# Layernorm's 1/sd by three Newton steps on GpSimd in place of ScalarE's square root, with half of efficient attention's applies on ScalarE

## Chip, cores and metric

The kernel runs on one core of one Trainium2 chip. The metric is the device time of one execution in microseconds, as the median of three runs. A core has a matrix engine (TensorE, PE in the profile), a vector engine (VectorE, DVE), an engine for activation functions (ScalarE, ACT), a general engine (GpSimd, POOL) and a queue engine for transfers (SyncE, SP). Each engine works through its own queue of instructions in order, and waits on semaphores for the others.

## What is computed

The input x is 8 batches of 512 tokens with 128 features. Six residual blocks follow one another, each behind a layernorm without weights:

```python
def _layernorm(x, axis=-1, eps=1e-05):
    m = jnp.mean(x, axis=axis, keepdims=True)
    v = jnp.var(x, axis=axis, keepdims=True)
    return (x - m) / jnp.sqrt(v + eps)

x = x + 0.5 * _L0_ffn_ref(_layernorm(x), ...)   # feed-forward, blockwise 4-bit values
x = x + _L0_attn_ref(_layernorm(x), ...)        # softmax attention, 16 heads of 64
x = x + 0.5 * _L0_ffn_ref(_layernorm(x), ...)   # the same feed-forward again
x = x + 0.5 * _L1_ffn_ref(_layernorm(x), ...)   # mixture of 8 experts, top 2
x = x + _L1_attn_ref(_layernorm(x), ...)        # efficient attention, 6 layers
x = x + 0.5 * _L1_ffn_ref(_layernorm(x), ...)   # the mixture again
```

Efficient attention is the stage that matters most here. Each of its six layers begins with a layernorm that has weights gamma and beta:

```python
for l in range(depth):
    residual = x
    h = _layernorm(x, gamma[l], beta[l])      # (x - mu) * rsqrt(var + 1e-5) * gamma + beta
    q, k, v = jnp.split(h @ w_qkv[l], 3, axis=-1)
    q = jax.nn.softmax(q, axis=1)             # over the tokens
    k = jax.nn.softmax(k, axis=2)             # over the features
    context = jnp.einsum('bic,bjc->bij', k, v)
    out = jnp.einsum('bic,bij->bjc', q, context) @ w_out[l] + b_out[l]
    x = out + residual
```

## The kernel before

All of x stays on the chip. Batch b is a tile xs[b] of 128 partitions by 4 chunks (NC) of 128 features: a token to a partition, four tokens a partition. The batches go in groups of four (GT). The six stages are functions that run in the order of the reference: ffn4, attention, ffn4, moe, linear_attention (the efficient attention), moe. The times of the stages in the profile are about 0 to 184, 184 to 1230, 1230 to 1369, 1369 to 1665, 1665 to 1971 and 1971 to 2271 us.

A scheduler arranges the instructions of an engine from their dependences and a cost model, so their order can differ from the order in the source. Tiles come from pools of a few buffers each; a tile with the same tag waits until the oldest buffer is free.

*Layernorm.* `ln_stats` (L152) takes the tiles of a group, 16 chunks in all. For each chunk VectorE makes the partial statistics st (bn_stats, L159) and from them mean and variance mv (bn_aggr, L161). Then one ScalarE instruction makes sd, the root of the variance plus eps (L163), and one VectorE instruction its reciprocal rstd (L165), each on 128x16. It is called 24 times: twice in each stage outside efficient attention, twice at the entry of efficient attention, and for each of its six layers and two groups. `ln_apply` (L168) then makes one VectorE instruction a chunk, 128x128: (x - mean) * rstd (L172), with the mean and rstd of each partition as operands.

ScalarE's functions live in tables. An ACT_TABLE_LOAD stands ahead of an instruction whose function isn't in the loaded one: ahead of Sqrt, of Exp, of the sigmoid functions.

*ffn4.* `hidden(t)` applies layernorm, quantizes xh (`quantize`, a chain on VectorE whose last multiplication, L214, is GpSimd's: x_xq, h_xq or w_xq), transposes it and makes the hidden values h. `down(t, h)` quantizes those and multiplies back. hidden(t + 1) is written ahead of down(t).

*attention.* A planner writes the order of TensorE's work by hand; `prepare(b)` makes a batch's layernorm and its transpose (L181), and GpSimd adds the bias bo to x (L322).

*moe.* The layernorm output mxh goes to memory, is gathered by GpSimd's indirect transfers for each expert, and the results are combined on VectorE.

*linear_attention.* `layer(l, batches, ys)` (L786) does one layer for one group of four batches; the layers run one after the other, the two groups in turn, so a group's layer is free to overlap with the other group's. This makes twelve layer-groups, here called periods. In each, for the four batches:

- xh is the applied layernorm (L172), 4 x 4 chunks; TensorE transposes it into ph (L798), ScalarE writes lhT with gamma and beta (L800), and GpSimd adds the output bias to y in place (L806), which must wait until xh has been read from y.
- TensorE multiplies to lpq (L812) and lpk (L825); VectorE takes the maxima nmq (L814) and nmk (L829); ScalarE's exponentials make eq (L817, 128x512) and ek (L833, 128x128 each).
- TensorE transposes eq (pqt, L845), VectorE scales it (eqt, L847), TensorE multiplies with ek to pm (L855), and VectorE scales that to mT (L859).
- A first round with w_out (pm2, L863) and a second with w_v (pm3, L868); behind each ScalarE copies the result, lm, out of PSUM (L865, L870), four copies a round.
- TensorE multiplies lhT with the second lm to lpo (L874, 16 instructions of two parts), and VectorE adds it to y (L877). In the last layer GpSimd adds y to x (L879).

The statistics of a group's next layer can begin once its y is added; its xh, ph and lpq follow while the other group is in its later steps. In the profile the y adds and the next ph of the group that is up stand side by side.

## Time and profile before

| what | value |
|---|---|
| median of 3 runs | 2272.65 us (2271.04 to 2274.14) |
| the profiled execution | 2272.8 us, its span 2271.1 us |
| instructions | 31365 |
| efficient attention, 1665 to 1971: PE, DVE, ACT, POOL busy | 268.9, 284.8, 194.3, 69.2 us of 306 |
| attention, 184 to 1230: PE, DVE, ACT, POOL busy | 1020.1, 675.3, 542.9, 46.7 us of 1046 |
| GpSimd's add of 128x512 (L806), 48 times | 1.286 us on average |
| GpSimd's scaling of x_xq 128x512 and h_xq 128x1408 (L214) | 1.341 and 2.684 us on average |
| VectorE's apply of 128x128 in efficient attention (L172), 192 times | median 0.338 us, up to 1.320 |

The span is the time from the first to the last instruction in the profile, and the execution's own time is 1.7 us more. In lines of the profile, "DVE L172 TENSOR_SCALAR xh<-y,mv,rstd 128x128 f32<-128x128 f32 x11" is eleven instructions of line 172 on VectorE that write xh from y, mv and rstd. In a timeline the first two numbers are the start and the busy time of a row in microseconds, and what stands in brackets at the end is how long the engine was idle before it and which instruction released it. In the view of one source line, the first row of each form has the shortest, median and longest duration in nanoseconds, with first and last start in microseconds. In the row of 40 slices each digit is the busy share in tenths; a slice is 56.8 us.

### The profile page before, as it was taken

Reading aid. Unit: us, or ns where it says so; the run is one execution under the profiler, and the core shown is the slowest. Engines: PE = TensorE matmul, PEld = TensorE weight load, DVE = VectorE, ACT = ScalarE, POOL = GpSimd, SP = SyncE. Lnnn points to the kernel's source line nnn. Section 1 sums busy time; section 2 is a strip of 40 time slices with the busy share of each in tenths; the row PEclk is TensorE's granted clock in tenths of the full one; section 3 lists DMA queues with packets and bytes.
Section 4 is the critical chain, followed back from the end, with each engine's and each line's share of the span. In section 5 each row is a group of like instructions: output and inputs, shape, how many; then the busy total and the mean of one; then the engine's idle time right before and its main releaser. Section 6 shows DMA issues by size and latency. Waiting matters only on the chain.

```text
span 2271.1 us, 31365 instructions
## 1 busy us (share of the span) xinstructions
PE 1869.2 (82%) x11321; PEld 1283.6 (57%) x11321; DVE 1509.5 (66%) x3392; ACT 946.5 (42%) x2439; POOL 467.3 (21%) x458
## 2 busy tenths in 40 slices
PE   2767999999999999999996755887439999859781
PEld 1544666665666566665664545654327777646560
DVE  8986756666575656666567994444379999745342
ACT  1324545555455545545451321232226767413230
POOL 1221000000000000000000220773332122227615
PEclk9888999999999999999998875797769999858885
DMA  6000000000000000000000001241100000013312
GB/s 175 1 0 1 1 1 1 1 1 1 1 1 1 1 1 1 1 1 1 1 1 1 1 0 37 56 93 48 48 18 1 1 1 1 20 35 74 85 58 65
DMA packets 57032, 47.61 MB, mean 21 GB/s; under 512 B 6512, under 2 KB 51760, under 8 KB 56880
## 3 DMA queue, kind: packets, MB, share of 16 engines
q1 hardware_dynamic: 46720, 26.16, 4.0%
q0 software_dynamic: 9216, 18.89, 3.8%
q8 instruction: 93, 1.52, 0.3%
q10 hardware_dynamic: 944, 0.54, 0.1%
q14 instruction: 59, 0.48, 0.1%
HBM read 28.80 MB, written 16.78 MB: 20 GB/s over the span
## 4 chain that ended last, share of the span: by engine, by line
PE 72%; DVE 14%; DMA 5%; issue 3%; POOL 3%; ACT 2%; POOLq 0%; DVEq 0%; ACTq 0%
PE pS L360 11%; PE pT L387 11%; PE po L402 10%; PE ph L690 5%; DMA yk<-yg,rows 4%; PE pym L714 3%; PE pq L332 3%; PE py L430 3%; PE pv L346 3%; PE pk L338 2%; PE ptok L629 2%; PE pm L855 2%; PE lpq L812 2%; PE lpo L874 2%; PE py L286 2%
## 5 line engine op out<-in xcount | busy, mean ns | idle before, releaser
L372 ACT ACTIVATE pe<-pS,nmax 128x512 f32<-128x512 f32 x512 | 348.7, 692 | 289.9 <-DVE nmax L369 216.3
L369 DVE TENSOR_REDUCE nmax<-pS 128x2 f32<-128x1024 f32 x256 | 302.0, 1218 | 131.6 <-PE pS L360 131.6
L392 DVE COPY aT<-pT 128x512 f32<-128x512 f32 x448 | 290.4, 684 | 97.5 <-PE pT L387 97.4
L387 PEld LDWEIGHTS pT<-ident,pe 128*128 128x128 f32 x2048 | 227.3, 141 | 86.6 <-issue 68.7
L387 PE MATMUL pT<-ident,pe 128*128 128x128 f32 x2048 | 273.1, 276 | 2.1 <-DVE aT L392 2.1
L360 PE MATMUL pS<-kT,qT 64*128 64x512 f32 x1024 | 256.4, 619 | 0.8 <-ACT pe L372 0.8
L402 PE MATMUL po<-aT,v 128*64 128x256 f32 x2048 | 249.6, 386 | 0.0
L414 POOL COPY wide<-rsum 128x512 f32<-128x512 f32 x64 | 39.3, 613 | 962.7 <-PE pT L387 903.8
L690 PE MATMUL ph<-wall,xgT 128*128 x320 | 166.3, 645 | 29.2 <-DVE g L696 21.7
L660 POOL DMA_INDIRECT xgs<-xg,toks x160 | 157.0, 981 | 157.7 <-DVE toks L634 109.5
L402 PEld LDWEIGHTS po<-aT,v 128*64 128x64 f32 x2048 | 136.2, 137 | 76.6 <-issue 21.3
L360 PEld LDWEIGHTS pS<-kT,qT 64*128 64x128 f32 x1024 | 88.6, 187 | 117.8 <-issue 109.4
L748 POOL DMA_INDIRECT yk<-yg,rows x128 | 120.9, 944 | 156.3 <-DMA yg<-ygs 111.0
L696 DVE TENSOR_TENSOR g<-g,ph 128x256 f32<-128x256 f32 x160 | 66.6, 419 | 112.3 <-ACT g L695 109.3
L695 ACT ACTIVATE g<-ph 128x256 f32<-128x256 f32 x160 | 60.9, 383 | 172.9 <-PE ph L690 172.9
L752 DVE SCALAR_TENSOR_TENSOR x<-yk,m,x 128x128 f32<-128x128 f32 x128 | 44.7, 353 | 118.6 <-DMA yk<-yg,rows 118.4
L806 POOL TENSOR_TENSOR y<-y,bout_sb 128x512 f32<-128x512 f32 x48 | 61.7, 1286 | 220.2 <-DVE xh L172 220.2
L372 ACT ACTIVATION_READ_ACCUMULATOR pe<-pS,nmax 128x1 f32 x512 | 105.8, 207 | 0.0
L690 PEld LDWEIGHTS ph<-wall,xgT 128*128 128x128 f32 x320 | 59.0, 207 | 79.9 <-issue 37.0
L277 PE MATMUL hqT_ps<-ident,h_xq 128*128 128x128 f32 (+1 forms) x192 | 35.1, 350 | 80.3 <-POOL h_xq L214 80.3
L798 PE MATMUL ph<-ident,xh 128*128 128x128 f32 x192 | 31.9, 295 | 72.6 <-DVE xh L172 72.5
L714 PE MATMUL pym<-wall,gT 128*128 x640 | 87.8, 296 | 1.4 <-DVE gT L707 1.4
(193 smaller groups left out, 3354.6 us busy)
## 6 DMA issues: line engine op xcount, KB each, us to landing
yg<-ygs SPq DMA_DIRECT2D x40, 256.0 KB, 2.4
xg<-mxh SPq DMA_DIRECT2D x16, 256.0 KB, 2.3
xgs<-xg,toks POOLq DMA_INDIRECT x160, 2.6
x<-in_x SPq DMA_DIRECT2D x8, 256.0 KB, 4.5
yk<-yg,rows POOLq DMA_INDIRECT x128, 2.5
out<-x SPq DMA_DIRECT2D x8, 256.0 KB, 2.5
wall<-in_w1T SPq DMA_DIRECT2D x1, 1024.0 KB, 9.2
wall<-in_w2T SPq DMA_DIRECT2D x1, 1024.0 KB, 11.5
```

The source lines that it names most:

```text
L332: nc.tensor.matmul(ps, wq_sb[:, cols(g)], hTs[g // NPAIR], start=True, stop=True)
L346: nc.tensor.matmul(ps[:, c, :], hT[:, c * P : (c + 1) * P], wv_sb[:, cols(g)], start=True, stop=True,)
L360: nc.tensor.matmul(ps[:, j, :], qTs[g][rows, c * P : (c + 1) * P], kTs[g][rows, :], start=True, stop=True,)
L369: nc.vector.tensor_reduce(nmax, ps, AX.X, ALU.max, negate=True)
L372: nc.scalar.activation(pe[:, j, :], ps[:, j, :], AF.Exp, bias=nmax[:, j : j + 1], accum_out=sums[g][:, 2 * c + j : 2 * c + j + 1],)
L387: nc.tensor.transpose(ps[:, k, :], pe[:, j, k * P : (k + 1) * P], ident)
L392: nc.vector.tensor_copy(dst, ps)
L402: nc.tensor.matmul(pos[g][rows, half * 2 * P : (half + 1) * 2 * P], vs[g][:, k, rows], aT[:, j, k, :], start=(k == 0), stop=(k == NC - 1),)
L660: nc.gpsimd.indirect_dma_start(x[:, s, :], None, xg[:, :], bass.IndirectOffsetOnAxis(ap=toks[:, q * QS + s : q * QS + s + 1], axis=0),)
L690: nc.tensor.matmul(ph.rearrange("p a h -> p (a h)"), xTs[q][:, s, :], wall[:, bass.ds(at, 2 * HID)], start=True, stop=True,)
L714: nc.tensor.matmul(py[:, s, :], gs[q][:, s, k, :], wall[:, bass.ds(ats[q * QS + s] + (2 * HID + k * D), D)], start=(k == 0), stop=(k == NH ...
L748: nc.gpsimd.indirect_dma_start(yk, None, yg[:, :], bass.IndirectOffsetOnAxis(ap=rows[:, j, k : k + 1], axis=0),)
```

## The change

The standard deviation's root and reciprocal go. In their place VectorE adds eps to the variance (v), shifts its bits to the right and subtracts them from a constant, which gives a first guess of 1/sqrt(v) by the form of floating-point numbers. GpSimd then multiplies v by -0.5 and does three Newton steps, each of four instructions on 128x16 that depend on one another: rstd = rstd * (1.5 - 0.5 * v * rstd * rstd). This is in `ln_stats`, so for all 24 layernorms. The tile eps, which was the bias of the root, goes too.

In efficient attention, a new function `ln_shift` makes -mean * rstd (one VectorE instruction on 128x16), and `ln_apply` gives every second chunk, 8 of the 16 of a group, to ScalarE as Identity with rstd as scale and the shift as bias. The applies of other stages stay on VectorE.

```diff
+RSQRT_GUESS = 0x5F3759DF
...
-    eps = const.tile([P, 1], F32, name="eps")
-    nc.vector.memset(eps, EPS)
...
-        sd = stat.tile([P, n], F32, name="sd", tag="sd")
-        nc.scalar.activation(sd, mv[:, :, 1], AF.Sqrt, bias=eps)
+
+        v = stat.tile([P, n], F32, name="v", tag="v")
+        nc.vector.tensor_scalar(v, mv[:, :, 1], EPS, None, ALU.add)
         rstd = stat.tile([P, n], F32, name="rstd", tag="rstd", bufs=3)
-        nc.vector.reciprocal(rstd, sd)
+        bits = stat.tile([P, n], I32, name="bits", tag="bits")
+        nc.vector.tensor_scalar(bits, v.bitcast(I32), 1, None, ALU.logical_shift_right)
+        nc.vector.tensor_scalar(rstd.bitcast(I32), bits, -1, RSQRT_GUESS, ALU.mult, ALU.add)
+        nc.gpsimd.tensor_scalar(v, v, -0.5, None, ALU.mult)
+        sq = stat.tile([P, n], F32, name="vsq", tag="vsq")
+        for _ in range(3):
+            nc.gpsimd.tensor_tensor(sq, rstd, rstd, ALU.mult)
+            nc.gpsimd.tensor_tensor(sq, sq, v, ALU.mult)
+            nc.gpsimd.tensor_scalar(sq, sq, 1.5, None, ALU.add)
+            nc.gpsimd.tensor_tensor(rstd, sq, rstd, ALU.mult)
         return mv, rstd
 
-    def ln_apply(dst, xt, stats, i):
+    def ln_shift(stats):
+
+        mv, rstd = stats
+        shift = stat.tile(rstd.shape, F32, name="shift", tag="shift")
+        nc.vector.scalar_tensor_tensor(shift, mv[:, :, 0], -1.0, rstd, ALU.mult, ALU.mult)
+        return shift
+
+    def ln_apply(dst, xt, stats, i, shift=None):
+
         mv, rstd = stats
         for c in range(NC):
             k = i * NC + c
+            if shift is not None and c % 2:
+                nc.scalar.activation(
+                    dst[:, c, :], xt[:, c, :], AF.Identity,
+                    bias=shift[:, k : k + 1], scale=rstd[:, k : k + 1],
+                )
+                continue
             nc.vector.tensor_scalar(
...
                 stats = ln_stats([ys[b] for b in batches])
+                shift = ln_shift(stats)
...
-                    ln_apply(xh, y, stats, i)
+                    ln_apply(xh, y, stats, i, shift)
```

## The prediction

> **What bounds the kernel now.** I read four views in order: the busy shares and slices of the page; the row of the square root with those who waited for it; the engines' timelines through one period of efficient attention, where half of the layernorms lie; and the chain of waits at the other layernorms.

> ```profile
> PE 1869.2 (82%) x11321; PEld 1283.6 (57%) x11321; DVE 1509.5 (66%) x3392; ACT 946.5 (42%) x2439; POOL 467.3 (21%) x458
> DVE  8986756666575656666567994444379999745342
> ACT  1324545555455545545451321232226767413230
> ```

> The shares average over six stages with different limits. Slices 30 to 34 are efficient attention (1665 to 1971 us): VectorE at 9, ScalarE at 6 to 7. There the change can act most.

> ```profile
> L163 ACT ACTIVATE sd<-mv,eps x24: 299/308/311, 17.1 to 1991.1; 128x16 f32<-128x16 f32 x24
> L163 ACT ACT_TABLE_LOAD  x20: 1283/1283/1283, 5.3 to 1961.1; - x20
>   DVE mv L161: 102.0, 19
>   PEld ph L798: 61.9, 1
>   DVE rstd L165: 5.4, 6
> ```

> 24 square roots of 0.31 us, with 20 table loads of 1.283 us. The last two lines list who waited: it is short, so most of these loads are not what another engine visibly waits for.

> Efficient attention runs twelve layer-groups, spaced 23.43 us (lpq at 1735.65 and 1759.08). ScalarE, VectorE and TensorE across the seam between two of them:

> ```profile
> 1747.46 1.28 ACT L163 ACT_TABLE_LOAD   x1
> 1749.41 0.31 ACT L163 ACTIVATE sd<-mv,eps 128x16 f32<-128x16 f32 x1 [0.67 <-DVE mv L161]
> 1750.17 0.27 ACT L865 COPY lm<-pm 128x128 f32<-128x128 f32 x1 [0.45 <-PE pm L863]
> ```
> ```profile
> 1750.21 0.24 DVE L165 RECIPROCAL rstd<-sd 128x16 f32<-128x16 f32 x1
> 1750.49 4.81 DVE L172 TENSOR_SCALAR xh<-y,mv,rstd 128x128 f32<-128x128 f32 x11
> 1755.23 0.68 DVE L877 TENSOR_TENSOR y<-lpo,y 128x512 f32<-128x512 f32 x1
> ```
> ```profile
> 1753.21 3.51 PE L874 MATMUL lpo<-lm,lhT 128*128 128x128 f32 x30
> 1758.65 0.59 PE L798 MATMUL ph<-ident,xh 128*128 128x128 f32 x2 [0.62 <-DVE xh L172]
> 1759.08 1.02 PE L812 MATMUL lpq<-lhT,wqkv_sb 128*128 128x512 f32 x2
> ```

> The period is a loop over three engines, and I cut it at E, the end of the last exponential (1747.44); S, the start of the long row of lpo (1753.21); and L, the next lpq (1759.08). E to S is 5.77, S to L 5.87, L to the next E 11.79 (23.43 in all). In E to S, the table load for the root ends at 1748.74, 0.67 before the last mean and variance (mv) is there: this load is hidden. The other load, back to exp at L817 (1737.79 to 1739.08), stands between the fourth lhT and the first exponential, and from there ScalarE runs without a gap to E: this load is on the path. VectorE applies eleven xh before the first y is added.

> [...]the trace has the 1.283[...] (load 1737.79, exponential 1739.08). [...]the new applies need no load; the trace's lm copies (L865) follow a root without one. [...]the trace has 1.06 us for 512 elements (x_xq) and 2.09 for 1120 (w_xq), 1.7 ns an element and 0.19 us at zero[...]. [...]a waiting ScalarE apply holds up the copies behind it.

> **The change part by part.** The profiled execution took 2272.8 (span 2271.1 and 1.7 around it), the median is 2272.65; so differences carry over as they are.

> *The price of a Newton step.* Each of the 24 calls of ln_stats gets three small VectorE operations (v, bits, guess), v times -0.5 on GpSimd beside bits and guess, and then 12 dependent GpSimd operations on 128x16. No row shows such an operation. From the slope: 0.19 + 16 x 0.0017 = 0.21 us; a hand-over from VectorE to GpSimd took 0.07 (y of L877 ended 1943.51, GpSimd began 1943.58), and I take the same for GpSimd waiting on itself: 0.28. Below: 0.20, when the dependent instruction's start overlaps its forerunner's end; the row of 32 numbers (iota) took 0.147. Above: 0.38, by the 128-element affine_select row (0.28) and a hand-over of 0.10. With 0.28 the chain is 12 x 0.28 = 3.36 (2.4 to 4.6); it replaces a root of 0.31 and a reciprocal of 0.24.

> *E to S, by the order in which the changed kernel issues.* mv is there at E+1.93, v at 2.13, the guess at 2.72 (an mT of 0.35 lies between), the Newton end at 6.08, shift (0.22) at 6.30. On ScalarE the first xh stands after the four copies of the first pm round and ahead of the four copies of the second, which lpo needs. So lpo now waits for Newton: hand-over 0.07, one xh spaced 0.33, one copy 0.27, hand-over 0.07: S = E+7.04, against 5.77: +1.27. The copies' own cover would last until E+5.8; what remains beyond it is the cost.

> *S to L.* Of 16 applies of a group ScalarE takes 8, so VectorE does six and not eleven ahead of the y adds, and they are done before the last lpo (3.51 after S). Then: hand-over 0.10, last y 0.67, one xh 0.34, hand-over 0.07, ph to lpq 0.38 (0.43 for two ph before): L = S+5.07, against 5.87: -0.80. What is late next is lpo itself. GpSimd's adds of bout_sb (1.29, L806) wait for both engines' applies; only the y adds wait for them, and they come later in this order.

> *L to E.* The load of 1.283 goes. Before, the first exponential began at L+3.43. Now nmq, which VectorE ended at L+1.75, allows it at L+1.8, but the fourth lhT (spaced 0.70) has moved inside the row of exponentials: 2.5 in its place, -0.9. So 10.9.

> Sum: +1.27 - 0.80 - 0.9 = -0.43 a period. Ten seams have it all: -4.3. The first and last layer-groups, which lose loads but have no full seam, -2 by estimate. GpSimd's 0.01 us more in price is 0.12 a period.

> *Outside efficient attention* (estimates from the rows around each layernorm; ScalarE applies nothing there):
> - First ffn4, group 0: Newton queues behind w_xq on GpSimd (16.84 to 18.93), rstd at 22.4 and not 19.2, of which 1.4 covers idle time: +2.2. Group 1: two loads and a root on ScalarE (68.14 to 71) go, Newton waits for h_xq (63.1 to 66.1): -1.
> - Attention's first layernorm (load at 161.11, on the chain): Newton behind the last h_xq, +1. Its second, at 719.5: two loads of 1.28 and a root stand on the chain of waits; GpSimd was idle for long, and TensorE has other heads' work: -2.
> - Second ffn4, group 1: h_xq holds GpSimd to 1260.3 and rstd was due at 1259.6, now 1263.6; one load saved: +2.5.
> - Entry to efficient attention +1 (Newton is exposed, but only half of layer 0's applies are VectorE's; 16 took 7.05 us). Mixture of experts: hidden in the first; +1.5 in the second pass, where mxh waits for GpSimd ahead of other VectorE work.

> Sum: 2.2 - 1 + 1 - 2 + 2.5 + 1 + 1.5 = +5.2. All: -4.3 - 2 + 5.2 = -1.1, so 2272 (2271.6). The three VectorE operations more a layernorm, against one reciprocal less, some 0.4 us, are in the times of v and guess; the applies taken off VectorE exceed them.

> **The rivals.** About six of the other layernorms and ten seams have Newton's 12 operations on the path: 16 x 12 = 192 operations, so 0.01 us of price is 1.9 us in all.

> *Newton is dearer* (the slower side): one mechanism, the GpSimd chain between mv and the lm copies, at 0.36 an operation, gives 192 x 0.08 = +15.4, so 2287. It decides from 0.31 up (1.9 x 3 - 1.1 = +4.6). For it: [...]small instructions above 0.2 in the trace (affine_select), and that GpSimd's 1.06 for 512 alone becomes 1.34 on average beside VectorE's work. Against it: memsets of one element took 0.10 to 0.12.

> *The loads and the split pay in full*: at 0.20 an operation E to S is 6.08, each seam gives 1.4, and all the rest shrinks too: -192 x 0.08 - 1.1 = -16.5, so 2256. For it: iota at 0.147; against it, the hand-over of 0.07.

> *The loads were hidden anyway*: if the first exponential waits for nmq or for TensorE, L to E gains only 0.3: +6 over ten seams, 2278. The row of exponentials without a gap behind the load speaks against it. I count it within the first case's own range.

> **How the numbers follow.** Break-even (2265 to 2279, by prices from 0.25 to 0.32): 0.45, and the likeliest, 2272. Newton dearer: 0.32. Paid in full: 0.23. About 0.2% (4.5 us) is what a measurement of this kernel tells from no change. Of the first case 0.14 falls below it, 0.21 within, 0.10 above; so faster 0.37, same 0.21, slower 0.42. The range reaches to 2256 and to 2290, which leaves a tenth out on each side; the first case's own is 2265 to 2279.

> **What would show it.** Table loads: 47 to 12, none left at a layernorm. GpSimd's 128x16 rows spaced 0.28, 24 x 13 of them. In a period: S at E+7.0, L at S+5.1, the first exponential 2.5 after L, and 23.0 as the spacing of lpq. The lm copies of the second round wait behind an xh that waits for shift, and lpo's idle is put down to them. ScalarE's apply 0.45 us; VectorE's applies 288 in place of 384. I am wrong if the Newton rows are spaced under 0.24 or over 0.32, if ScalarE's queue doesn't hold lpo, or if another stage moves by more than 4 us.

## The result and the profile after

The changed kernel takes 2294.38 us (median of 4 runs, 2292.7 to 2295.42), the kernel before, measured beside it, 2271.85. The ratio is 1.0099, with a 95% interval of 1.0082 to 1.0117: about 22 us slower. A second measurement (after_again) gave 2294.23 and 1.0086 (1.0069 to 1.0103). In the profiled executions the spans are 2291.0 and 2271.1, a difference of 19.9, which is what the traces have to explain.

The changed kernel has 12 table loads (1.283 us each) in place of 47, as forecast, and none of them is at the new applies. Its page has the shares and slices. The line of the square root is gone, and two views of lines in its place show the last GpSimd instruction of a Newton step and the shift that waits for it:

```profile
PE 1869.5 (82%) x11321; PEld 1293.8 (56%) x11321; DVE 1477.6 (64%) x3355; ACT 931.1 (41%) x2476; POOL 539.9 (24%) x770
DVE  8996666566666666666667983544377778645342
ACT  1224545455454545455451221332046666403230
```
```profile
L174 POOL TENSOR_TENSOR rstd<-vsq,rstd x72: 220/222/223, 20.6 to 2012.5; 128x16 f32<-128x16 f32 x72
L181 DVE SCALAR_TENSOR_TENSOR shift<-mv,rstd x12: 174/175/176, 1682.2 to 1957.8; 128x16 f32<-128x16 f32 x12
  POOL rstd L174: 38.3, 12
```

VectorE does 32 us less and ScalarE 15 less. Still efficient attention's slices have VectorE at 7 to 8 where they had 9. One cause is that half of the applies there have left VectorE. The last line shows the other: twelve times, once a layer-group, VectorE stood still for 3.2 us on average until the Newton chain had ended.

By landmarks the 19.9 us lie as follows; a "row of exponentials" is that of one layer-group, twelve in each kernel.

| stretch of the profiled execution, us | before | after | difference |
|---|---|---|---|
| up to the first mixture (first mxh) | 1369.50 | 1369.28 | -0.2 |
| first mixture, to its last write of x | 296.02 | 292.84 | -3.2 |
| entry of efficient attention, to the end of the first row of exponentials | 33.47 | 40.57 | 7.1 |
| from there to the end of the twelfth row | 262.07 | 275.04 | 13.0 |
| behind it | 310.04 | 313.24 | 3.2 |

The prediction had 3.7 ahead of the layers, -6.3 in them (some of this at their edges) and 1.5 behind. So most of the error lies in the seams between the layer-groups, and about 6 us more at the entry. There nothing covers Newton, twice, ahead of TensorE's first product of the stage: once for the entry's second layernorm, and once for layer 0's.

```profile
1671.52 4.19 DVE L195 TENSOR_SCALAR y<-x,mv,rstd 128x128 f32<-128x128 f32 x16 [2.22 <-POOL rstd L174]
1682.15 0.17 DVE L181 SCALAR_TENSOR_TENSOR shift<-mv,rstd 128x16 f32<-128x16 f32 x1 [2.21 <-POOL rstd L174]
```

The shorter mixture isn't shown to be the change's: e8_behind_copies and e15_behind_held below, with the same code there, have 296.06 and 296.43.

One seam of the changed kernel, with E (the end of the last exponential) at 1751.95. First the timeline of GpSimd and VectorE (start, busy time, engine, line, operation; in brackets the idle time ahead and its releaser):

```profile
1754.71 0.22 POOL L171 TENSOR_TENSOR vsq<-rstd 128x16 f32<-128x16 f32 x1
1755.00 0.22 POOL L172 TENSOR_TENSOR vsq<-vsq,v 128x16 f32<-128x16 f32 x1
1755.31 0.26 POOL L173 TENSOR_SCALAR vsq<-vsq 128x16 f32<-128x16 f32 x1
1755.65 0.22 POOL L174 TENSOR_TENSOR rstd<-vsq,rstd 128x16 f32<-128x16 f32 x1
...
1758.13 0.22 POOL L174 TENSOR_TENSOR rstd<-vsq,rstd 128x16 f32<-128x16 f32 x1
```
```profile
1758.38 0.17 DVE L181 SCALAR_TENSOR_TENSOR shift<-mv,rstd 128x16 f32<-128x16 f32 x1 [3.33 <-POOL rstd L174]
1758.48 1.62 DVE L195 TENSOR_SCALAR xh<-y,mv,rstd 128x128 f32<-128x128 f32 x6
1762.32 0.69 DVE L901 TENSOR_TENSOR y<-lpo,y 128x512 f32<-128x512 f32 x1 [2.22 <-PE lpo L898]
```

The twelve instructions from 1754.71 to 1758.35 are spaced 0.31 on average. Then the timelines of ScalarE and TensorE in the same seam:

```profile
1756.48 0.27 ACT L889 COPY lm<-pm 128x128 f32<-128x128 f32 x1 [0.35 <-PE pm L887]
1758.65 0.49 ACT L190 ACTIVATE xh<-y,shift,rstd 128x128 f32<-128x128 f32 x1 [1.91 <-DVE shift L181]
1759.05 0.41 ACT L894 COPY lm<-pm 128x128 f32<-128x128 f32 x2
```
```profile
1756.28 1.01 PE L892 MATMUL pm<-lm,wvT_sb 128*128 128x128 f32 x4
1759.35 1.23 PE L892 MATMUL pm<-lm,wvT_sb 128*128 128x128 f32 x4 [2.07 <-ACT lm L894]
1760.37 4.65 PE L898 MATMUL lpo<-lm,lhT 128*128 128x128 f32 x32
1766.32 1.13 PE L836 MATMUL lpq<-lhT,wqkv_sb 128*128 128x512 f32 x2
```

ScalarE's first xh waits 1.91 us, two lm copies stand behind it, and TensorE is idle for 2.07. Behind the copies it has first to make two more products of the second round (pm3 has two buffers, so they could not go ahead of the copies), and only then lpo. And the 32 instructions of lpo take 4.65 us. The view of windows (start and end, length, busy time of TensorE, its weight loads, VectorE, ScalarE and GpSimd; behind them TensorE's granted clock, DMA share, GB/s) has the same stretch and another seam of the same kernel, and in its third line all eleven seams of the kernel before:

```profile
1760.37:1765.00 4.63, 4.63 (x35) 4.63 (x35) 2.65 (x7) 1.89 (x6) 3.36 (x3) 0.79 0.01 4
1836.33:1840.00 3.67, 3.67 (x35) 3.67 (x34) 2.74 (x7) 2.01 (x6) 3.64 (x3) 1.00 0.00 0
1692.00:1960.00 268.00, 248.71 (x1717) 202.39 (x1717) 254.52 (x867) 183.03 (x634) 61.55 (x48) 1.00 0.00 1
```

35 matmuls take 4.63 us at a clock of 0.79 and 3.67 at 1.00. The clock is 0.50 for 3.4 us (6.8 in the first case) behind the wait in seven of the eleven seams (1732, 1760, 1787, 1811, 1886, 1910, 1961), and 1.00 in the other four, of which three have the same wait (the first seam has none). The kernel before has no seam with a lower clock. The distances between the ends of the exponentials follow this: 23.96 to 23.98 in three of the nine inner seams, 25.35 to 25.60 in five with the fall, 26.62 in one where it lasted longest; before, 23.42 to 23.56 in all nine.

| pieces of a seam, us | before | forecast | after, clock 1.00 (E 1828.38) | after, clock falls (E 1751.95) |
|---|---|---|---|---|
| E to the long row of lpo | 5.77 | 7.04 | 7.95 | 8.42 |
| from there to lpq | 5.87 | 5.07 | 5.04 | 5.95 |
| lpq to the next E | 11.79 | 10.9 | 10.99 | 10.98 |
| sum | 23.43 | 23.0 | 23.98 | 25.35 |

### The profile page after: what moved, and what is told of

Its sections match the earlier page's. It is cut to its first block, busy times and chain, and to the rows that moved or that the text cites. A ratio compares the mean times of both kernels' runs of the same rounds, so it can differ in the third digit from the quotient of the medians.

```text
span 2291.0 us, 31656 instructions
## 1 busy us (share of the span) xinstructions
PE 1869.5 (82%) x11321; PEld 1293.8 (56%) x11321; DVE 1477.6 (64%) x3355; ACT 931.1 (41%) x2476; POOL 539.9 (24%) x770
## 4 chain that ended last, share of the span: by engine, by line
PE 66%; DVE 13%; ACT 6%; POOL 6%; DMA 5%; issue 3%; POOLq 0%; DVEq 0%; ACTq 0%
PE pS L383 11%; PE pT L410 11%; PE po L425 10%; PE ph L713 5%; DMA yk<-yg,rows 4%; PE pym L737 3%; PE pq L355 3%; PE py L453 3%; PE pv L369 3%; PE pk L361 2%; PE lpo L898 2%; PE ptok L652 2%; ACT ek L857 2%; PE pr L204 2%; PE py L309 1%
## 5 line engine op out<-in xcount | busy, mean ns | idle before, releaser
L425 PEld LDWEIGHTS po<-aT,v 128*64 128x64 f32 x2048 | 135.8, 136 | 77.0 <-issue 21.3
L737 PEld LDWEIGHTS pym<-wall,gT 128*128 128x128 f32 x640 | 83.6, 210 | 4.3 <-DVE gT L730 2.3
```

The costliest lines, as they stand in the source:

```text
L425: nc.tensor.matmul(pos[g][rows, half * 2 * P : (half + 1) * 2 * P], vs[g][:, k, rows], aT[:, j, k, :], start=(k == 0), stop=(k == NC - 1),)
L737: nc.tensor.matmul(py[:, s, :], gs[q][:, s, k, :], wall[:, bass.ds(ats[q * QS + s] + (2 * HID + k * D), D)], start=(k == 0), stop=(k == NH ...
```

## The experiments

All edits are to the changed kernel where nothing else is said. "Period" is the distance between the ends of two rows of exponentials. An order is set with dependences between instructions of one engine that have no wait of their own (NOSYNC; HELD is a real wait). "..." in a cut of code stands for what is left out. Ratios are to the kernel before, measured beside each; stretches of a trace are of one profiled execution.

**The copies freed (e8_behind_copies).** ScalarE's applies are put behind the last lm copy of the other group.

```diff
-                nc.scalar.activation(
+                ins = nc.scalar.activation(
...
+                if behind:
+                    tc.add_manual_dep(ins.ins, behind[0], ...)
...
+                    ln_apply(xh, y, stats, i, shift, behind=list(last_lm))
```

> The changed kernel with one difference: ScalarE's eight applies of a layer-group stand behind the second round of lm copies in its queue, not among them. Theory A (the place in ScalarE's queue is the loss: lpo waits for Newton through the copies, and TensorE's clock falls after that wait): lpo starts 5.2 us after the last exponential and not 8.0 to 8.4, TensorE's clock stays at 1.00 in the seams, the period is 21.3 to 22.5 and not 24.0 to 25.5, and the whole 2250 to 2268. Rival B (Newton's latency itself decides, through xh, ph and lpq): lpo starts early but ph and lpq wait, the period stays at 24 or above, the whole is 2285 or more.

Measured: 2290.61 us, ratio 1.0072 (1.0054 to 1.0090), hardly below the changed kernel. Six of the eleven periods are 23.73 to 23.76. lpo starts as early as in the kernel before (its long row at E+6.02), and in nine of the eleven seams the clock holds (it falls to 0.50 for 3.4 us at 1866.84 and at 1965.84); but the period is nearly what it was. Theory A's first part came true and its sum didn't; the whole is in rival B's range, though the period isn't. VectorE's and GpSimd's timelines of this kernel, in a seam with E at 1756.46:

```profile
1762.89 0.17 DVE L181 SCALAR_TENSOR_TENSOR shift<-mv,rstd 128x16 f32<-128x16 f32 x1 [3.32 <-POOL rstd L174]
1762.98 3.78 DVE L197 TENSOR_SCALAR xh<-y,mv,rstd 128x128 f32<-128x128 f32 x6
1766.68 0.68 DVE L906 TENSOR_TENSOR y<-lpo,y 128x512 f32<-128x512 f32 x1
```
```profile
1764.12 2.56 POOL L834 TENSOR_TENSOR y<-y,bout_sb 128x512 f32<-128x512 f32 x2 [1.26 <-DVE xh L197]
```

Two things hold the first y add at E+10.2, as late as before the mend (E+10.4). VectorE's own queue has the y adds behind the shift, so the wait for Newton is paid a second time, in another queue. And the six applies take 3.78 and not 1.62 us, since GpSimd's additions of b_out now start while they run.

**The wait filled (e9_filled).** TensorE's wait gets two products of constants, with the order of all other instructions as in the changed kernel.

```diff
+                    if i == 2 and (l, batches[0]) != (DEPTH - 1, GT):
+                        for _ in range(2):
+                            fill = misc.tile([P, TT], F32, name="fill", tag="misc")
+                            ins = nc.tensor.matmul(fill, ident, wall[:, :TT], start=True, stop=True)
...
```

> The changed kernel with its own order on all engines, and two multiplications of constants (128x512, about 0.9 us each, result unused) put into TensorE's wait between the second and the third pm3 of each layer-group but the last. Theory A (part of the loss is that the clock granted to TensorE halves after this wait in seven of eleven seams): no slice of efficient attention below clock 0.98, every period at 23.9 to 24.1, the whole 8 to 12 us below the changed kernel: 2282 to 2286. Rival C (the lower clock costs nothing because lpo isn't what ends the seam): 2293 to 2296.

Measured: 2286.99 us, ratio 1.0057 (1.0039 to 1.0075), so 7 to 10 us below the changed kernel by the two ratios. All nine inner periods are 23.94 to 23.97, and the row from the first to the twelfth layer-group is 266.44 us in place of 275.04: 8.6 less, by adding work. The whole is just above the range that was expected: in the first seam, which had no wait to fill, the products cost 1.9. The first line is a window that holds the wait and the lpo of one seam of this kernel, the second its timeline:

```profile
1751.00:1765.00 14.00, 13.45 (x98) 11.22 (x99) 9.20 (x38) 6.13 (x24) 6.74 (x16) 1.00 0.01 1
```
```profile
1758.05 2.21 PE L900 MATMUL fill<-wall,ident 128*128 128x512 f32 x4
```

The products fill the wait (2.21 us), the clock is 1.00, and lpo takes 3.74. That the fall of the clock is a cost of its own is shown: some 8 us of the loss.

**Newton without the split (e1_newton_no_split).** All applies on VectorE, `ln_apply(xh, y, stats, i)`.

> Newton on GpSimd in all layernorms, but all applies on VectorE. ScalarE's copies are then free of Newton. Theory A: lpo starts 5.2 after the last exponential and the clock stays up, but the applies (sixteen on VectorE from 6.5 on) and y adds come late; period 23 to 25, the whole 2270 to 2290, below the changed kernel. Rival D (the GpSimd chain costs the same wherever it is waited for, the split only helps): the whole above the changed kernel, 2296 to 2310.

Measured: 2329.79 us, ratio 1.0247 (1.0225 to 1.0269), inner periods 27.57 to 28.95: worse by more than rival D said. The scheduler places an xh ahead of each y add, so VectorE waits 3.78 us for Newton with the y adds behind it, and then has up to twelve applies left (in one seam ten, which take 5.12 beside GpSimd's additions); TensorE's clock falls to 0.50 for 3.4 or 6.8 us in all eleven seams. The split is not what loses.

**Newton on VectorE (e3_newton_vector).** The 13 instructions as `nc.vector`.

> All 13 instructions of the Newton steps on VectorE in place of GpSimd, applies split as in the change. The scheduler then puts the applies of ScalarE behind the lm copies. Theory A: the chain is 12 x 0.2 = 2.5 us of VectorE, no queue holds lpo, the clock stays up; period 22 to 23.5, the whole 2255 to 2272. Rival B (any Newton chain of this length between mv and xh loses): 2285 or more.

Measured: 2303.91 us, ratio 1.0129 (1.0102 to 1.0156), far above the 2255 to 2272 of theory A and in rival B's range. The instructions are spaced 0.21 and not 0.31, as expected, but the scheduler puts the applies between and behind the y adds, where they meet GpSimd's additions (five take 3.33 us) and TensorE waits for them; most periods are 24.6. The first row of exponentials ends 15.1 us later than in the changed kernel, but not by what happens at the entry, which is 3.1 us shorter: 13.5 us of it are there at the start of the first mixture (1382.76 against 1369.28), most of them from the second ffn4. What holds that stage up stays open.

**The additions of b_out left out (e10_behind_no_bias)**, on top of e8. In this measurement, and in the next three (e11, e12, e2), the mixture stages were longer for every kernel (the kernel before took 2437.89 us); efficient attention's rows have the durations of the other measurements, so here the periods and ratios count.

> As e8_behind_copies, with GpSimd's 48 additions of b_out in efficient attention left out. Theory N (Newton's latency holds VectorE's queue: shift waits 3.3 us, and applies and y adds stand behind it; what e8 gained at the copies it lost because GpSimd's additions then ran beside VectorE's six applies, which took 3.78 and not 1.62 us): without the additions the six applies take 1.6 to 1.8 again, the first y add starts 8.0 to 8.4 after the last exponential and not 10.2, the period is 21.5 to 22.4, the whole 2266 to 2275. Rival (the additions cost nothing, something else ends the seam): period 23.5 or more, the whole 2285 or more.

Measured: ratio 0.9981 (0.9975 to 0.9988), period 22.80, against e8's 23.74 and 24.9. The six applies are back at 1.62 and the first y add at E+8.1, so the collision costs 0.9 or more a seam. The expected period, 21.5 to 22.4, asked too much.

**One Newton step (e11_behind_one_step)**, on top of e8: `range(1)`, which leaves 1/sd less exact.

> As e8_behind_copies, with one Newton step in place of three in all layernorms (so 1/sd is only good to about 0.2%). Theory N: eight GpSimd instructions of 0.30 us less, 2.4 us a seam and in the six exposed layernorms outside; period 21.2 to 22.2, the whole 2250 to 2265. Rival (the chain's length is covered): the whole 2280 or more.

Measured: ratio 0.9914 (0.9897 to 0.9930), period 22.26 to 22.28. Eight GpSimd instructions less (2.5 us) shorten the seam by 1.5. The chain's length counts, at some 60%; the rest had other cover.

**The chain under the exponentials (e12_early).** mv, v, bits and guess (first_rstd) go ahead of the other group's first eqt on VectorE.

```diff
+                tc.add_manual_dep(last_eqt[0], first_rstd[0], NOSYNC, reason="order")
```

> The changed kernel, with only the place of mv, v, bits and guess on VectorE moved: ahead of the other group's first eqt, so that the 13 GpSimd instructions run under the exponentials; all work is the same. Theory N: shift waits 0 to 0.7 and not 3.3 us, TensorE has no long wait and its clock stays at 1.00, lpo starts 5.2 to 6.2 after the last exponential, period 21.3 to 22.5, the whole 2256 to 2270, below the kernel before. Rival (GpSimd's Newton costs by its contention with VectorE, or the split costs, wherever it stands): 2283 or more.

Measured: ratio 1.0160 (1.0143 to 1.0177), inner periods 25.6 to 27.2, the opposite of theory N. The wait of shift did fall to 0.68. But the scheduler now puts applies between the mT, and these applies met GpSimd's additions. TensorE's timeline of this kernel:

```profile
1868.78 0.49 PE L896 MATMUL pm<-wout_sb,mT 128*128 128x128 f32 x2 [0.21 <-DVE mT L892]
1871.94 1.33 PE L896 MATMUL pm<-wout_sb,mT 128*128 128x128 f32 x6 [2.67 <-DVE mT L892]
```

It waits 2.67 us for an mT behind three applies of 2.98, and its clock is 0.50 from 1873.52 to 1876.92. The wait that went came back one place further up, with a fall of 3.4 us behind it.

**The split alone (e2_split_root).** Root, reciprocal and loads as in the kernel before, with shift and ScalarE's applies.

> ScalarE's half of the applies alone: root, reciprocal and table loads as before the change. Theory N (the split is a gain, Newton the loss): VectorE's queue has five applies less ahead of the y adds; period 22.2 to 23.3, the whole 2256 to 2270. Rival (the split is part of the loss, since ScalarE's applies stand ahead of the lm copies): period 23.5 or more, the whole 2274 to 2285.

Measured: ratio 0.9970 (0.9960 to 0.9981), period 22.96 in all inner seams, 0.47 less than before. The split is a gain by itself; so in the order that the scheduler gives, Newton is the loss.

**The additions held back.** GpSimd's additions of b_out wait for the first nmq of their layer-group, so that they run beside the exponentials: on top of e8 (e15_behind_held), on top of the split alone (e15_split_root_held), and as the only edit to the kernel before (e15_before_held).

```diff
+                    for add in adds:
+                        tc.add_manual_dep(add, ins.ins.name, HELD, reason="hold")
```

> As e8_behind_copies (applies behind the copies), and GpSimd's additions of b_out wait for the first nmq of their layer-group, so that they run beside the exponentials and not beside VectorE's applies; all work is kept. Theory N (collision of these additions with VectorE's applies took back the gain of e8): six applies take 1.6 to 1.8 and not 3.8 us, period 22.6 to 23.0 and not 23.74, ratio to the kernel before 0.999 to 1.003. Rival (held back, the additions cost as much elsewhere): period 23.5 or more, ratio 1.006 or more.

> As e2_split_root (split alone, root and loads kept), with the additions of b_out held back until nmq. If the collision counts here too: the last four applies of a group take 1.2 and not 3.1 us; period 21.8 to 22.6 and not 22.96, ratio 0.990 to 0.995. If ScalarE's loads or TensorE end the seam: 22.9 and 0.997.

> The kernel before with only the additions of b_out held back until nmq. If the collision counts there: eleven applies take 3.1 to 3.5 and not 4.81 us, period 22.3 to 23.1 and not 23.43, ratio 0.994 to 0.998. If y adds wait for lpo anyway: 23.4 and 1.000.

Measured: e15_behind_held 2274.70 us, ratio 1.0003 (0.9994 to 1.0012), period 22.76 to 22.78; e15_split_root_held 2258.45 and 0.9934 (0.9914 to 0.9954), but with its period still at 22.96, as the second half of its expectation said, while the ratio is that of the first half; why its ratio is lower than e2's isn't explained. e15_before_held 2256.66 and 0.9928 (0.9911 to 0.9944), period 22.62 to 22.64, a larger gain than expected. VectorE's timeline of e15_behind_held (E at 1780.01) and of e15_before_held:

```profile
1786.45 0.18 DVE L182 SCALAR_TENSOR_TENSOR shift<-mv,rstd 128x16 f32<-128x16 f32 x1 [3.32 <-POOL rstd L175]
1786.54 1.62 DVE L198 TENSOR_SCALAR xh<-y,mv,rstd 128x128 f32<-128x128 f32 x6
1788.08 0.69 DVE L912 TENSOR_TENSOR y<-lpo,y 128x512 f32<-128x512 f32 x1
```
```profile
1767.56 2.91 DVE L173 TENSOR_SCALAR xh<-y,mv,rstd 128x128 f32<-128x128 f32 x11
```

Six applies are back at 1.62, the first y add at E+8.1. In the kernel before, eleven applies take 2.91 in place of 4.81. The collision is shown, in the old kernel too. Of the 16.3 us between the two spans 9.6 lie between the first and the twelfth row of exponentials and 2.1 at the entry, where these additions stand; the other 4.6 lie where none does, most of them in the second mixture, and are not explained. By what mechanism the applies slow down beside GpSimd, no run here shows. For these additions VectorE alone is slowed: their median is 1.29 in the kernel before, where they run beside applies, and 1.28 in the changed kernel, where in the seams they don't.

**Early and held (e16_early_behind_held)**, then **with shift and applies behind all mT, and the guess ahead of the third eqt (e17_early_behind_all)**.

> As e15_behind_held, and mv to guess are placed ahead of the other group's first eqt, so that GpSimd's Newton runs under the exponentials. All work of the changed kernel is kept. Theory N (the wait of shift for Newton, with applies and y adds behind it on VectorE, is the rest of the loss): shift waits at most 0.7 us, period 21.3 to 22.3, ratio to the kernel before 0.991 to 0.997. Rival (Newton on GpSimd costs in itself, by contention): period 22.8 or more, ratio 1.000 or more.

> As e16_early_behind_held, with shift and VectorE's applies placed behind all four mT (in e16 two mT stood behind the shift that waits for Newton, and TensorE waited for them), and the guess ahead of the third eqt, not the first. All work of the changed kernel is kept. Theory N (a place in VectorE's queue decides what Newton costs): shift waits under 0.5 us, lpo starts 5.2 to 6.0 after the last exponential, period 21.3 to 22.2, ratio to the kernel before 0.984 to 0.992. Rival (another 1 us or more of Newton's cost stays wherever it stands): period 22.7 or more, ratio 1.000 or more.

Measured: e16 2283.37 us, ratio 1.0049 (1.0032 to 1.0066), period 23.48; e17 2261.58 us, ratio 0.9952 (0.9937 to 0.9968), period 22.32 to 22.34. Both fall short of what theory N expected; e16 is where its rival was. In e16 two mT stood behind the shift, which still waited 0.67, and six applies. In e17 nothing that TensorE needs stands behind it:

```profile
1837.48 0.35 DVE L908 TENSOR_SCALAR mT<-pm,rq 128x128 f32<-128x128 f32 x1 [0.57 <-PE pm L904]
1838.48 0.18 DVE L187 SCALAR_TENSOR_TENSOR shift<-mv,rstd 128x16 f32<-128x16 f32 x1 [0.64 <-POOL rstd L178]
1838.57 1.62 DVE L205 TENSOR_SCALAR xh<-y,mv,rstd 128x128 f32<-128x128 f32 x6
1841.62 0.69 DVE L928 TENSOR_TENSOR y<-lpo,y 128x512 f32<-128x512 f32 x1 [1.42 <-PE lpo L925]
```

The y add waits for lpo, not for an apply. All work of the change, done in other places, is faster than the kernel before. But its additions are held back too: against the kernel before with its additions held (0.9928) e17 isn't faster. It is 5.8 us shorter from the first to the twelfth row of exponentials (246.61 against 252.44), and 5.3 longer at the entry (36.61 against 31.35).

**Root against Newton in equal places (e15_root_behind_held, against e15_behind_held).**

> As e15_behind_held in every place, but with root, reciprocal and table loads in place of Newton. Theory N (in equal places, Newton's 3.3 us of wait outweigh the loads): period 21.9 to 22.6 and not 22.78, and no layernorm outside pays: ratio to the kernel before 0.986 to 0.993. Rival (in equal places the two cost the same): period 22.7 to 23.0, ratio 0.994 to 0.998.

Measured: 2262.52 us, ratio 0.9956 (0.9940 to 0.9973), period 23.13 to 23.16. In the seams I was wrong: with copies free and additions held, Newton's 22.78 is below the root's 23.15. From the first to the twelfth layer-group the two take the same, 254.98 and 255.04. Nearly all of the difference in the whole lies ahead of this: the first row of exponentials ends at 1709.14 with Newton and at 1694.77 with the root. Of these 14.4 us 10.1 are at the entry (40.63 against 30.50) and 3.8 ahead of the first mixture. As the two kernels differ in nothing but Newton and root, this is what Newton costs outside the seams, in these two executions.

**Newton inside the layers only (e18_newton_inside, against after_again)**, with root and reciprocal in the twelve calls outside them, and **the same on e17 (e19_inside_placed)**.

> The changed kernel with Newton only in the layers of efficient attention; the twelve layernorms outside them keep root and reciprocal. By the landmarks of the traces these lost 4 to 5 us of the whole: below the changed kernel in the same call by 3 to 6 us. Rival (all of the loss is inside): within 1.5 us of it.

> The changed kernel again, for the comparison within this call: ratio to the kernel before 1.008 to 1.012 on a chip with the times of the first call; seams of 24.0 where TensorE's clock holds and 25.4 to 25.6 where it falls.

> As e17_early_behind_all in efficient attention's layers, with root and reciprocal kept in the twelve layernorms outside them. If the layernorms outside carry 4 to 9 us of Newton's cost and the layers are as in e17: period 22.3, ratio to the kernel before 0.988 to 0.993, below e17's 0.9952 and the lowest of all, with e15_before_held (0.9928) the one to beat. Rival (outside, placed or not, Newton costs nothing): 0.995.

Measured: e18 2285.54 us, ratio 1.0048 (1.0031 to 1.0065), against 1.0086 (1.0069 to 1.0103) for after_again: 8.7 us less by the medians, 4.7 by the spans. e19 2253.70 us, ratio 0.9936 (0.9915 to 0.9957), period 22.33. So the layernorms outside carry several us of Newton's cost in the changed kernel. Where, these two traces can't tell well: e18 is 4.3 us shorter up to the first mixture, 2.5 at the entry and 6.5 behind the layers, but its first mixture took 300.6 us where all others of the usual length have 292.8 to 297.5. For e19 against e17 (0.9952) the intervals overlap, so there the gain isn't told apart from none, though the first row of exponentials ends 2.7 us earlier. e19 and e15_before_held are about level, some 16 us below the kernel before.

## Why the prediction was wrong

*The piece S to L* (forecast 5.07, measured 5.04) and *the piece L to E* (10.9, 10.99) were right where the clock held: the load ahead of the exponentials did stand on the path, and the split does shorten what stands ahead of the y adds.

*The price of a Newton step* was near: from the end of the guess (1754.60) to the end of the chain (1758.35) are 3.75 us and not 3.36, so 0.31 for 0.28. That is just the point from which the rival "Newton is dearer" was to decide. The rival named the right place, the chain between mv and the lm copies, and 2287 as the time; but at the prediction's own rate of 1.9 us for 0.01 its price gives 6 us, of a loss of 22.

*E to S is the step that failed*, forecast at E+7.04. Even with the clock up it is 7.95: 0.3 of the 0.9 is the chain (shift ends at E+6.60 and not 6.30), nearly all of the rest the term that I left out between the first lm copy and lpo, two more products of the second round, 0.55 (1835.78 to 1836.33), which had to wait for the copies because pm3 has two buffers. I had let lpo start with the first copy. These 0.9 turn the forecast -0.43 a period into +0.5.

*The term that was missing* is what TensorE's idle time does to its clock. I counted the wait of 2 us as a wait, and not that in seven of eleven seams 3.4 us or more then run at a clock of 0.50. The inner seams with the fall are 1.4 to 2.7 longer than those without; e9 shows 8.6 over the layers. The forecast has no term for the clock, which in the profile before is at 1.00 through all seams. The nine inner seams are 15.0 longer together, three by 0.5 each and six by 1.9 to 3.2; the first seam is 2.4 shorter, as the forecast's -2 for the edges had it, and the last 0.4 longer.

*Where the wait stands* went with whether the clock fell. In the traces of the kernel before and of the changed kernel every change of the clock (51 and 63 of them) lies a whole number of 3.41 us behind the one before it, and so do, to 0.05 us, the 86 changes that were read in windows of 2 us in ten more runs. The first three lines below are three such steps of 3.41 us in a row in the seam with E at 1751.95, where the wait began 1.84 us into the first of them; the last is the step that holds most of the wait in the seam with E at 1828.38, where the wait began 3.17 us into the step before:

```profile
1755.45:1758.86 3.41, 1.57 (x10) 1.00 (x8) 0.48 (x3) 0.96 (x4) 2.16 (x10) 1.00 0.00 0
1758.87:1762.27 3.40, 2.92 (x13) 2.92 (x14) 1.23 (x5) 2.91 (x10) 1.83 (x2) 0.50 0.00 0
1762.28:1765.68 3.40, 3.40 (x33) 3.40 (x32) 3.33 (x8) 0.33 (x2) 1.95 (x2) 1.00 0.02 5
1833.96:1837.36 3.40, 1.58 (x14) 1.58 (x15) 1.72 (x7) 2.26 (x8) 1.64 (x4) 1.00 0.00 0
```

The changed kernel has this wait ten times, 2.01 to 2.07 us long. The clock held behind the three that began 3.17 to 3.25 us into a step, and fell behind the other seven, which began 1.59 to 2.52 us into one, or 3.27 to 3.33. In after_again and e18 the clock was read behind eighteen more of these waits (their starts are estimates: 1.31 us ahead of ScalarE's first xh in the first and 1.37 in the others, as in the changed kernel). It held behind six that began 3.17 to 3.25 us into a step, and fell behind twelve that began 0.5 to 2.7 us into one, or 3.30 to 3.33. So in these traces which of the seams paid went with where they happened to stand.

*That VectorE's queue waits as well* was not seen: the forecast had the shift's wait on ScalarE's queue alone, and took the y adds for done in time. e8 shows that freeing ScalarE's queue gives nearly nothing while the shift stands ahead of the y adds on VectorE.

*GpSimd's additions*: the forecast said that only the y adds wait for them. What counts is that VectorE's applies slow down beside them. In the seams of the changed kernel they were by chance apart (six applies in 1.62), so this is no part of the loss there; it decided what each mend of it gave.

*Outside the layers* the sum fits by luck. Up to the end of the first row of exponentials 3.7 were forecast and 3.7 measured, but as -0.2 up to the first mixture (forecast 2.7; the second trace of the same kernel has 2.4), -3.2 in the mixture (forecast 0, and not the change's as far as is shown) and 7.1 at the entry. The entry is the second step that failed, and by the prediction's own sign, a stage that moves by more than 4 us. The forecast of +1 has Newton exposed there, with fewer applies on VectorE against it. The trace has it exposed twice, ahead of the second half of the entry's layernorm and again ahead of layer 0's, and in kernels otherwise equal Newton's entry is 10.1 longer than the root's. Behind the layers 1.5 were forecast and 3.2 measured.

One reading was off, and nothing rests on it: in the slices of the page VectorE's 9 and ScalarE's 6 to 7 are slices 31 to 34; slice 30 is mostly the mixture.

What stays open: what of TensorE's work in a step goes with a fall. Its busy time in the step ahead of a fall and in one behind which the clock held is the same in the lines above (1.57 and 1.58 us). No run here moved the wait on purpose.

## What to carry to other kernels

Before a wait is put on an instruction, list for every engine that gets one what stands behind it in that engine's queue: here the same wait was paid by ScalarE's copies, by VectorE's y adds and, in one experiment, by mT, and freeing one queue alone gave little (1.0072 for 1.0099). Where such a wait leaves TensorE idle for some us, add the stretch at a lower clock that can follow it to the cost (here 3.4 us or more at 0.50 behind seven of ten waits of 2 us), and look at the granted clock in short windows; filling the gap with idle work is a cheap test of it. Where a sum comes out right, compare its terms by landmarks in more than one trace: here two errors of some us cancelled. And where GpSimd and VectorE work on SBUF at the same time, look at the duration of one VectorE instruction with and without company: holding back 48 GpSimd additions, with no other edit, took 16 us off the kernel before, about 12 of them where the additions stand.
